# Leaving out some of GpSimd's clears between row gathers in a two-layer graph kernel

## The chip, the cores and the metric

The kernel runs on one core of one Trainium2 chip. The metric is the device time of one execution in microseconds. The core's engines run side by side, each through its own queue in order: TensorE (PE; its weight loads are shown as PEld), VectorE (DVE), ScalarE (ACT), GpSimd (POOL) and SyncE (SP). They wait for each other through semaphores. Time before: 2917.17 us, the median of 14 runs (2896.22 to 2936.71).

## The reference

16 graphs of 1024 nodes with 64 features each. Layer 0 adds a small network over `adj @ x` and normalizes. Layer 1 thins each node's neighbours and takes, feature by feature, a weighted sum of three quantiles over the neighbours that stay; then comes a network of two matrices and a normalization.

```python
# layer 0
messages = einsum('bij,bjh->bih', adjacency, h)
dh = tanh(concat([h, messages]) @ W1 + b1) @ W2 + b2
x = layernorm(x + dh)
# layer 1: which neighbours stay
nb = (adj > 0) & ~eye;  m = nb.sum(-1);  rank = cumsum(nb) - 1
skip = where(m > 10, (m + 1) // 2, 1)
removed = nb & (skip > 1) & mask & ((rank + 1) % skip == 0)
valid = adj_with_self_loops & ~(removed | removed.T)
# layer 1: quantiles of each feature over the valid neighbours
sv = sort(where(valid, x[neighbour], big))
agg = sum(w * interpolated(sv, tau) for tau, w in ((.25, .25), (.5, .5), (.75, .25)))
y = relu((x + agg) @ W1 + b1) @ W2 + b2
x = layernorm(x + y * mask)
```

## The kernel before, in words

The function `sparse` does all the work for inputs within its limits. (`general` is a slower form that runs only if a flag says that the input is outside; it did not run here.)

The graphs are taken in six sets: one, one, two, four, four and four graphs (sets 0 to 5). The nodes of a set are put in order of their number of neighbours, most first, and cut into tiles of 128 nodes, one node to a partition. The front does this for one graph after another: VectorE scores the adjacency tiles (`score`), ScalarE counts, TensorE transposes tiles and forms the messages, layer 0 follows (its rows go to tables in DRAM), and `places` finds each node's place in the order (`perm`). Then the heads of a set, its nodes with most neighbours, are fetched (`permuted`), their lists of neighbours made on VectorE, the removed neighbours picked, and the removals scattered by GpSimd into the tables (`table<-removes`).

After that the kernel goes through units, 47 in all. A unit is a tile, or up to four, with the same room for neighbours; `index4_8` in what follows is the unit of set 4 that begins with tile 8. For each unit:

- `fetches` calls `fetch_rows` (line 1124): for each neighbour place GpSimd issues one indirect DMA, a gather, that brings for each of 128 nodes the row (66 floats) of one neighbour into the tile `X`. After every third gather GpSimd clears a scratch tile of 128x384 bytes, `pause`, that nobody reads.
- `prepare`: VectorE and ScalarE put large values in empty places and find the quantile's weights.
- `sort`: VectorE runs a sorting network over the neighbour places, `tensor_tensor` with min or max between `X` and a second tile `Y`, so both inputs are in SBUF.
- `sum_up` and `finish`: ScalarE weights the sorted places, TensorE adds them up and applies the network, VectorE normalizes, and GpSimd scatters the result (`out_dram<-y`) with an indirect DMA.

There are four `X` tiles, so GpSimd may be up to four units ahead. Lists for later tiles of a set are made while units run; their `permuted` fetches are on GpSimd's queue too, two buffers at a time. The nodes with most neighbours of all (hubs) have units of their own. The two greatest classes, with 50 and 156 gathers (tiles `pair` and `X0`, here the great hubs), are fetched by `great_fetches` and sorted by `great_units`. They use memory that the front frees, and their lists (`hub_list`, `hub_sc`, then `hub_ix`) are made on VectorE once the heads of all sets are done.

The order of instructions on each engine is fixed when the program is built. The work is written as 19 jobs, generators that yield between steps (`run_jobs`). A planner, `Board`, keeps for each engine the modelled time at which it is free, and for each tile when it is written and read. Every call of an instruction goes through the class `Engine`, which adds a modelled cost: 1600 ns for an indirect DMA on GpSimd, 1.2 ns a byte for a clear (461 ns), and for VectorE 145 ns and a cycle an element. At each step the job that can start first by this model, with a bias for each job, goes on. So a changed cost or a left-out instruction on one engine can change the order on every engine. All calls pass through one helper, so nearly every instruction has the same line in the profile (316); it is told apart by its tiles.

Of the kernel before, what the change touches and what calls it, by code (L numbers as in the profile page):

```python
# [228 lines left out]
class Board:  # L229


    def __init__(self):
        self.free = dict.fromkeys("VATGS", 0.0)
        self.written, self.read = {}, {}
        self.mark = 0.0
        self.moved = 0.0
        self.table = None


class Engine:  # L240
# [34 lines left out]
    def __getattr__(self, name):  # L275
        op, board, key = getattr(self.engine, name), self.board, self.key

        def timed(*args, **kw):
            out = kw.get("out", args[0] if args else None)
            rest = list(args[1:] if "out" not in kw else args) + list(kw.values())  # L280
            func = next((a for a in rest if isinstance(a, type(AF.Tanh))), None)
            ins = [a for a in rest if isinstance(a, bass.AP) and a is not out]
            outs = [out] + [a for k, a in kw.items() if k == "accum_out" and a is not None]
            for k in ("in_offset", "out_offset"):
                if kw.get(k) is not None:
                    ins.append(kw[k].ap)
            start = board.free[key]
            for t in ins:
                if t.space != DRAM:
                    start = max(start, board.written.get(t.tensor.name, 0.0))  # L290
            for t in outs:
                if t.space != DRAM:
                    start = max(start, board.read.get(t.tensor.name, 0.0))
            cost = self.cost(name, out, ins, dict(kw, func=func))
            end = start + cost
            board.free[key] = end
            if key != "G" and "dma" in name:
                big = out if out.space != DRAM else ins[0]
                size = big.free_nbytes() * big.partition_size()
                board.moved = max(board.moved, start + LANDS) + size / 200  # L300
                end = board.moved + LANDS
                board.free[key] = start + cost
            elif key == "G" and "dma" in name:
                big = max([out] + ins, key=lambda t: 0 if t.space == DRAM else t.free_nbytes())
                size = big.free_nbytes() * big.partition_size()
                board.moved = max(board.moved, end) + size / 200
                end = board.moved + 2 * LANDS
            else:
                end += 100
            for t in ins:  # L310
                board.read[t.tensor.name] = max(board.read.get(t.tensor.name, 0.0), end)
            for t in outs:
                if t.space != DRAM:
                    board.written[t.tensor.name] = max(board.written.get(t.tensor.name, 0.0), end)
            board.mark = max(board.mark, end)
            return op(*args, **kw)  # L316

        return timed
# [47 lines left out]
def sparse(ctx, tc, x, adj, nodemask, w1a, b1a, w2a, b2a, w1b, b1b, w2b, b2b, consts, out,  # L366
# [5 lines left out]
    board = Board()  # L372
    V, A, T, GP, SY = (Engine(e, k, board) for e, k in zip(
        (nc.vector, nc.scalar, nc.tensor, nc.gpsimd, nc.sync), "VATGS"))
# [30 lines left out]
    pause = cp.tile([P, PAUSE], U8, name="s_pause")  # L405
# [718 lines left out]
    def fetch_rows(u, src):  # L1124

        X, n = u["X"], 0
        for k, cap in enumerate(u["caps"]):
            SY.dma_start(X[:, 0, k, :], u["own_rows"][k])
            for d in range(1, cap + 1):
                GP.indirect_dma_start(out=X[:, d, k, :], out_offset=None, in_=src,  # L1130
                                      in_offset=bass.IndirectOffsetOnAxis(
                                          ap=u["index"][k][:, d - 1:d], axis=0))
                n += 1
                if n % 3 == 0:
                    GP.memset(pause, 0.0)
                    yield "G", 0

    def check_limits(pool):
# [55 lines left out]
    def fetches(pool):  # L1194
        for i, (si, c, what) in enumerate(plan):
            yield "G", lambda i=i, si=si: i in units and done["heads"] > si
            if i >= XBUFS:
                yield "G", lambda i=i: done["free"] > i - XBUFS
            u = units[i]
            u["X"] = pool.tile([P, u["caps"][0] + 1, len(what), W], F32, tag="X", name="X",  # L1200
                               bufs=XBUFS)
            src = table
            if c is None:
                src = early[si] if si < len(early) else tables[SETS[si][0] // 4]
            elif c > 3:
                src = tables[0]
            yield from fetch_rows(u, src)
            done["fetch"] += 1
# [38 lines left out]
    def great_fetches():  # L1247


        yield "S", lambda: "pool" in late  # L1250
        pool = late["pool"]
        check_limits(pool)
        for c in (1, 0):
            late[c] = yield from hub_lists(pool, c, [0], "great_sc")
        for c in (1, 0):
            u = late[c]
            D = u["caps"][0] + 1
            yield "G", 0
            if c:
                pair = pool.tile([P, 2, D, 1, W], F32, tag="Y0", name="pair")  # L1260
                u["X"], u["Y"] = pair[:, 0], pair[:, 1]
            else:
                u["X"] = pool.tile([P, D, 1, W], F32, tag="X0", name="X")
            yield from fetch_rows(u, table)
            late["fetched"] = c
# [566 lines left out]
```

## Time and profile before

| what | value |
|---|---|
| median of 14 runs | 2917.17 us (2896.22 to 2936.71) |
| the profiled execution | 2935.83 us, span 2934.1 us |
| gathers into X and pair | 1238 |
| scatters and list fetches on GpSimd: out_dram, permuted | 122, 128 |
| clears (s_pause) | 402, mean 439 ns, 176.4 us in all |
| first `perm` to last | 74 to 1113 us |
| last head's removals scattered | 1307 us |
| great hubs: 50 gathers, then 156 | 1360 to 1428, 1429 to 1705 us |
| last gather ends | 2863 us |

The page is of one execution; its times are not the median's. A row of the page names engine, operation, output tile and inputs, then the count, the busy time, the mean of one, and the idle time of the engine before it with what ended it. "Issue" is a gap in which the engine waited for nothing that the profile shows. The indirect DMAs have rows on POOL for the time in which GpSimd prepares them; their landing is another matter.

The sort steps' own rows overlap a little, since VectorE starts one step before the one ahead has ended. A 128x256 step has a row of 0.42 us and follows the one before it by about 0.34.

### The profile page before, as it was taken

The page shows a single profiled execution, that of the slowest core. Times are in us where ns is not written, and L with a number is a line of the kernel's source. Part 1 is how long each engine was busy: PE and PEld are TensorE (multiplying, and loading weights), DVE is VectorE, ACT ScalarE, POOL GpSimd, SP SyncE. Part 2 cuts the span into 40 slices and gives each one's busy share as a digit, 9 for nine tenths or more (in the row PEclk, how much of TensorE's full clock was granted, in tenths as well). Part 3 has the DMA queues.
Part 4 walks back from the last instruction along what each step waited for, and adds up shares of the span by engine and source line. Part 5 has one row for each costly group of instructions (what it writes and reads, how often), then busy time and mean ns, then how long its engine had stood idle before and what let it go on. Part 6 is the DMA issues. An engine that isn't in the chain of part 4 may idle for free.

```text
span 2934.1 us, 23546 instructions
## 1 busy us (share of the span) xinstructions
PE 1260.9 (43%) x4992; PEld 790.3 (27%) x4992; DVE 1987.4 (68%) x5189; ACT 1248.0 (43%) x3739; POOL 1924.7 (66%) x1955
## 2 busy tenths in 40 slices
PE   6786757756686674210233002221124421103376
PEld 4453434434443332200123001121012221102155
DVE  3467877575678686769994005878889786688752
ACT  5685676554777554222222026222225322123364
POOL 1035835777524575767688883878888888888882
PEclk9897867856786776555555555555555555555555
DMA  7476545234445342311111111122111122121110
GB/s 242 150 211 168 154 128 151 56 85 113 126 140 163 94 122 52 64 29 35 20 22 22 25 26 44 38 46 51 23 23 24 26 51 43 28 58 27 24 25 8
DMA packets 158610, 215.63 MB, mean 73 GB/s; under 512 B 88524, under 2 KB 88716, under 8 KB 158460
## 3 DMA queue, kind: packets, MB, share of 16 engines
q0 software_dynamic: 56192, 87.29, 14.5%
q1 hardware_dynamic: 83836, 93.20, 11.2%
q10 hardware_dynamic: 18432, 33.56, 3.1%
q14 instruction: 108, 0.88, 0.1%
q8 instruction: 42, 0.69, 0.1%
HBM read 157.21 MB, written 56.70 MB: 73 GB/s over the span
## 4 chain that ended last, share of the span: by engine, by line
POOL 38%; PE 16%; DVE 16%; issue 15%; ACT 9%; DMA 3%; another core or an unknown queue 2%; SPq 0%; POOLq 0%; DVEq 0%; ACTq 0%
POOL X L316 30%; PE pn L316 6%; ACT junk L316 5%; POOL s_pause L316 4%; POOL out_dram L316 3%; PE pt L316 3%; DVE Y L316 3%; PE pa L316 3%; DVE X L316 2%; ACT X L316 2%; PE rows L316 2%; DVE hub_list L316 2%; DVE score L316 2%; DVE hub_sc L316 1%
## 5 line engine op out<-in xcount | busy, mean ns | idle before, releaser
L316 POOL DMA_INDIRECT X<-table,index x711 | 808.0, 1136 | 210.9 <-issue 188.8
L316 ACT ACTIVATE X<-X,fill 128x64 f32<-128x64 f32 x1188 | 304.9, 336 | 498.1 <-DVE fill L316 415.3
L316 PE MATMUL pa<-X,s_half_ident 128*128 128x64 f32 (+3 forms) x636 | 202.4, 467 | 561.3 <-ACT X L316 461.9
L316 POOL DMA_INDIRECT X<-table,hub_ix x262 | 317.5, 1212 | 69.7 <-issue 69.4
L316 POOL DMA_INDIRECT permuted<-score_rows,ids x128 | 143.7, 1122 | 325.1 <-DMA early<-s_rows 112.3
L316 PE MATMUL pa<-Y,s_half_ident 128*128 128x64 f32 (+2 forms) x522 | 174.1, 478 | 369.0 <-ACT Y L316 223.7
L316 PEld LDWEIGHTS pa<-X,s_half_ident 128*128 128x128 f32 x636 | 141.7, 298 | 623.1 <-ACT X L316 511.2
L316 POOL DMA_INDIRECT X<-early,index x215 | 224.9, 1046 | 93.3 <-issue 56.0
L316 PE MATMUL pn<-aT,x_sb 128*64 128x256 f32 x1024 | 279.8, 421 | 5.1 <-issue 4.8
L316 DVE TENSOR_TENSOR Y<-X 128x512 f32<-128x512 f32 (+11 forms) x414 | 248.2, 625 | 8.9 <-PE pt L316 6.4
L316 ACT ACTIVATE X<-X,wt 128x64 f32<-128x64 f32 x614 | 162.9, 336 | 195.7 <-DVE X L316 195.3
L316 POOL DMA_INDIRECT out_dram<-y,out_ids x122 | 142.4, 1167 | 145.5 <-DVE y L316 80.3
L316 PEld LDWEIGHTS pa<-Y,s_half_ident 128*128 128x128 f32 x522 | 118.6, 302 | 418.2 <-ACT Y L316 250.9
L316 PE MATMUL pt<-s_ident,a_sb 128*128 128x128 f32 x1024 | 166.5, 309 | 135.4 <-ACT aT L316 82.4
L316 DVE SCALAR_TENSOR_TENSOR score<-a_sb,s_desc 128x1024 f16<-128x1024 f32 x128 | 155.0, 1222 | 94.5 <-DMA score_rows<-score 47.2
L316 DVE TENSOR_TENSOR X<-Y 128x256 f32<-128x256 f32 (+10 forms) x377 | 212.4, 582 | 2.5
L316 ACT ACTIVATE Y<-Y,wt 128x64 f32<-128x64 f32 x530 | 141.9, 336 | 146.0 <-DVE Y L316 125.1
L316 ACT COPY aT<-pt 128x512 f32<-128x512 f32 x256 | 138.7, 583 | 142.0 <-PE pt L316 65.4
L316 PEld LDWEIGHTS pt<-s_ident,a_sb 128*128 128x128 f32 x1024 | 136.4, 197 | 180.0 <-ACT aT L316 97.0
L316 POOL MEMSET s_pause<- 128x384 uint8 x402 | 176.4, 439 | 3.0 <-remote 2.8
L316 PEld LDWEIGHTS pn<-aT,x_sb 128*64 128x64 f32 x1024 | 143.0, 150 | 107.3 <-issue 49.7
L316 ACT ACTIVATE junk<-keys,nkey 128x1024 bf16<-128x1024 f32 x128 | 142.5, 1113 | 26.6 <-DVE nkey L316 6.5
(181 smaller groups left out, 2904.5 us busy)
## 6 DMA issues: line engine op xcount, KB each, us to landing
a_sb<-in_adj_dram SPq DMA_DIRECT2D x128, 512.0 KB
score_rows<-score ACTq DMA_DIRECT2D x128, 256.0 KB
X<-table,index POOLq DMA_INDIRECT x711
score_rows<-s_rows SPq DMA_DIRECT2D x16, 264.0 KB
table<-s_rows SPq DMA_DIRECT2D x16, 264.0 KB
X<-table,hub_ix POOLq DMA_INDIRECT x262
x_sb<-in_x_dram SPq DMA_DIRECT2D x16, 256.0 KB
own_rows<-permuted SPq DMA_DIRECT2D x122, 33.0 KB
```

The lines of the kernel that those rows point to most:

```text
L316: return op(*args, **kw)
```

## The change

The planner keeps a list of the modelled start and end of every `tensor_tensor` on VectorE. Where a clear would be issued it looks at the 6000 ns that end at VectorE's modelled time. If `tensor_tensor` fills more than half of them, and GpSimd's modelled time is less than 6000 ns ahead of VectorE's, the clear is left out. Otherwise it is issued as before. The job still yields after every third gather.

```diff
@@ class Board
         self.table = None
+        self.pairs = []
+
+    def paired(self, span=6000):
+        now, total = self.free["V"], 0.0
+        for start, end in reversed(self.pairs):
+            if end <= now - span:
+                break
+            total += end - max(start, now - span)
+        return self.free["G"] - now < span and total > 0.5 * span
@@ class Engine, timed
             board.free[key] = end
+            if key == "V" and name == "tensor_tensor":
+                board.pairs.append((start, end))
@@ fetch_rows
                 n += 1
                 if n % 3 == 0:
-                    GP.memset(pause, 0.0)
+                    if not board.paired():
+                        GP.memset(pause, 0.0)
                     yield "G", 0
```

## The prediction

> **What bounds the kernel now.** I read the page's engine rows and slices first, then windows over the stages, then single instructions. The profiled execution took 2935.83 us (span 2934.1). It lies near the top of the 14 runs, 0.64% above their median of 2917.17, so I work out a difference against it and put that difference on the median.
>
> ```profile
> span 2934.1 us, 23546 instructions
> PE 1260.9 (43%) x4992; PEld 790.3 (27%) x4992; DVE 1987.4 (68%) x5189; ACT 1248.0 (43%) x3739; POOL 1924.7 (66%) x1955
> ...
> DVE  3467877575678686769994005878889786688752
> ...
> POOL 1035835777524575767688883878888888888882
> ...
> POOL 38%; PE 16%; DVE 16%; issue 15%; ACT 9%; DMA 3%; another core or an unknown queue 2%; SPq 0%; POOLq 0%; DVEq 0%; ACTq 0%
> ```
>
> Over the whole span no engine is full, but from slice 24 on GpSimd (POOL) stands at 8 in every slice but the last, and it leads the chain that ended last. The stages (columns: PE, PEld, DVE, ACT, POOL busy, with instruction counts):
>
> ```profile
> 0.00:1080.00 1080.00, 743.59 (x3277) 442.87 (x3277) 715.19 (x2019) 669.57 (x1545) 525.20 (x564) 0.77 0.50 141
> 1080.00:1360.00 280.00, 79.81 (x373) 56.44 (x372) 205.19 (x681) 87.33 (x278) 187.13 (x202) 0.58 0.25 50
> ...
> 1429.00:1565.00 136.00, 54.46 (x143) 32.77 (x144) 130.99 (x279) 48.86 (x190) 104.53 (x85) 0.53 0.10 19
> 1565.00:1707.00 142.00, 18.10 (x76) 14.44 (x74) 7.14 (x27) 12.50 (x48) 114.80 (x140) 0.52 0.12 25
> ...
> 1830.00:2863.00 1033.00, 302.87 (x906) 198.96 (x906) 806.77 (x1905) 325.54 (x1281) 857.09 (x809) 0.52 0.18 35
> ```
>
> Two facts follow. Before 1080 us GpSimd waits a lot; afterwards it hardly does. In 1830 to 2863 it is busy 857 of 1033 us, and nearly all the rest is a gap of 0.30 us ahead of each gather, which is issue and not a wait. Counting only gaps above that 0.30 us, it is idle for 431 us before 1080, 50 in 1080 to 1360, 14 in 1429 to 1565, 39 in 1707 to 1830 and 6 until 2863. So from 1080 on the end moves with the sum of GpSimd's work, until about 71 us of sums and output remain after the last gather (2863). VectorE (DVE) follows: it is at 78% in the last long stage and idle in 1565 to 1707.
>
> **What a clear costs.** In a stretch without sorting:
>
> ```profile
> 1642.10 0.94 POOL L316 DMA_INDIRECT X<-table,hub_ix  x1 [0.30 <-issue]
> 1643.35 0.95 POOL L316 DMA_INDIRECT X<-table,hub_ix  x1 [0.30 <-issue]
> 1644.30 0.43 POOL L316 MEMSET s_pause<- 128x384 uint8 x1
> 1644.89 0.95 POOL L316 DMA_INDIRECT X<-table,hub_ix  x1 [0.16 <-issue]
> ```
>
> From 1642.10 to 1643.35 is one gather to the next, 1.25 us. With a clear between, 1643.35 to 1644.89, it is 1.54 us. So a clear costs 0.29 us and not the 0.44 us of its row: its own time takes the place of one 0.30 gap, and the gap after it is 0.16.
>
> **Part 1, clears removed.** In the two programs' GpSimd orders there are 402 clears before and 172 after, 230 fewer. By stage of the new order: 25 fewer ahead of the great hubs' gathers (units up to index3_5), 34 of 68 fewer among the great hubs' 206 gathers, 12 fewer in index3_8, 3_12 and 3_16, and 159 of 188 fewer from index3_20 to the end. The first 25 lie mostly before 1080 where 431 us of waits cover them: nothing, and a gain of 7 us if that cover were gone. The other 205 x 0.29 = **-60 us**.
>
> **Part 2, what VectorE does to gathers.**
>
> ```profile
> L316 POOL DMA_INDIRECT X<-table,hub_ix x56 | 83.7, 1494 | 14.9 <-issue 14.9
> L316 POOL MEMSET s_pause<- 128x384 uint8 x18 | 7.9, 438 | 0.0
> ```
> ```profile
> L316 POOL DMA_INDIRECT X<-table,hub_ix x100 | 95.1, 951 | 25.9 <-issue 25.9
> L316 POOL MEMSET s_pause<- 128x384 uint8 x34 | 14.8, 436 | 0.0
> ```
> ```profile
> 1527.83 19.34 DVE L316 TENSOR_TENSOR pair<-pair 128x256 f32<-128x256 f32 x63
> 1527.93 0.44 POOL L316 MEMSET s_pause<- 128x384 uint8 x1
> 1528.53 17.67 POOL L316 DMA_INDIRECT X<-table,hub_ix  x1 [0.16 <-issue]
> ```
>
> The first pair is 1429 to 1565 with VectorE sorting, the second 1565 to 1707 with it idle, the third one gather held for 17.67 us by 63 sort steps. Gathers are stretched (1494 against 951 ns); clears are not (438 against 436). Sort steps are not slowed by gathers: a 128x256 step takes 421 ns with a gather beside it throughout (231 of them) and 421 with GpSimd idle (27). So VectorE neither gains nor loses here. Does a clear spare the next gather some of the stretch? Over all unit gathers with sorting beside at least 90% of their time, the first after a clear takes 1543 ns (115 of them), the second 1389 (125), the third 1308 (123). It does not, so I count the 0.29 in full; the bound on the other side is that half of it comes back as longer gathers (+30).
>
> The Trainium skill (SBUF — State Buffer, section Who interferes with whom) says that a VectorE instruction with two SBUF inputs locks out a GpSimd instruction that reads SBUF, but not one that only writes. That fits these rows and speaks against the change: the clear is the one thing in this queue that a sort cannot delay, so its time might only become waiting for the port. By that rule alone, with all 205 given back, the sum below would be +30 and 2947 us; by the row it is -30.
>
> **Part 3, the planner moves work.** Removing clears changes the planner's GpSimd time and so every engine's order. The largest move: the great hubs' gathers (50 and 156 rows) now stand ahead of index3_8, 3_12 and 3_16 (90 gathers). They need VectorE's lists of the great hubs, behind the last heads of set 5. Before, GpSimd had those 90 gathers to do meanwhile (58+54+37 us of fetch spans in 1191 to 1360). Now it has little, and in its queue everything stands behind the great gathers: the 90 rows that VectorE sorts next, list fetches, and scatters of results.
>
> When are the lists ready? I add each VectorE instruction at its mean duration along both orders. From the last placement tile (1113 us) to the 50 rows' index (1350) VectorE had 178 us of work in 237 us, 75% busy. In the new order it is 129 us, as the sorts of index3_1 to 3_5 are put after it, and the placement comes some 13 us sooner. At 75%: 1100 + 172 = 1272. Bounds: 1229 with VectorE always busy, 1350 if nothing comes sooner. GpSimd has 95 us of work for 1080 to 1272 (280 less 50 idle less some 135 for the 90 gathers, their clears, stretch and scatters), so it idles 97 instead of 50: **+47 us**, between +4 and +125. The second index comes 47 us of VectorE work later, 63 at 75%, as long as the 50 gathers take (50 x 1.25 + 14 x 0.29 = 67): no second wait.
>
> Coming back: the 39 us idle in 1707 to 1830 is mainly one wait, for list buffers while VectorE was held at the great hubs' first step:
>
> ```profile
> POOL permuted L316 <- DVE lists L316: 37.5, 3, 30.3
> ```
>
> With 90 more gathers (113 us) ahead of that point VectorE can catch up: **-30 us**, between 0 and -39. The 14 us wait for a scatter stays.
>
> The 90 gathers change company: their stretch was 9 us in 1170 to 1360; beside the great hubs' sort I take the late stage's rate (151 us of stretch over 587 gathers from 1707 on, 0.26 each): 23 us, so **+14 us**, between 0 and +41 (the 0.56 of 1429 to 1565).
>
> SyncE's issues for each unit's own rows go with the units and the list transfers change place alike; SyncE is no share of the chain (SPq 0%). ScalarE has four table loads fewer and TensorE the same instructions; both are at 43% or below: nothing. VectorE has the same instructions. If its cover went, that is if VectorE were late for gathered units, the late stage has 1033 - 807 = 226 us of room, against 46 us (159 x 0.29) by which that stage shrinks.
>
> **Sum.** -60 + 47 - 30 + 14 = -29 us: 2936 becomes 2907, and 2917 becomes **2888** (0.990).
>
> **The rivals.**
> A, the sum: about 2888, its own range 2862 to 2910. Chance 0.50.
> B, the great hubs' gathers take the place of the clears as the wait. GpSimd stands at the first of the 50 gathers until VectorE has the lists; each us later than 1272 is one us at the end. From 1301 on nothing is gained, from 1316 on the kernel is slower by over 0.5%. At 1335, with VectorE's waits unshortened: -29 + 63 = +34, 2951 us. For it: VectorE's waits in 1080 to 1360 are partly for other engines. Against: GpSimd fetches the heads sooner with nothing between. 0.22.
> C, half of the clears' time comes back as stretched gathers: -29 + 30, 2918 us. For it the 17.67 us row, against it the places after a clear. 0.15.
> D, the planner's new order suits: lists at 1229, the list wait gone, no added stretch: -60 + 4 - 39 + 0 - 7 = -102; I put it at 2830. 0.13.
> That the change does nothing is excluded by the count of clears; 42% stay.
>
> **How the numbers follow.** About 0.5% (15 us) is what a measurement can tell from no change. Faster: 0.42 of A, all of D, 0.03 of C = 0.58. Same: 0.08 of A, 0.09 of C, 0.03 of B = 0.20. Slower: 0.19 of B, 0.03 of C = 0.22. Range: 2838 to 2955, from just short of D's 2830 to just past B's 2951, some 0.10 left out on either side.
>
> **What would show it.** Clears 172; gather to gather 1.25 us still; the 50-row gathers starting near 1272 with GpSimd idle before them, the 156-row ones ending near 1595 (1705 before); index3_20 starting near 1744 (1707 + 47 + 14 - 46 x 0.29, less 11 for 8 scatters that move behind it); no list wait of 30 us behind it; the last gather some 30 us sooner. I am wrong if the 50 rows start after 1301 (step 3), if the gathers' mean in the late stage rises above 1.3 us from 1.23 (step 2), or if VectorE gets over 90% busy there.

## The result, and the profile after

The changed kernel takes 3049.3 us (median of 10 runs, 3028.82 to 3071.45) where the kernel before takes 2920.2 us beside it: a ratio of 1.0466 [1.0435, 1.0497]. It is slower by 4.7%, and the time lies above the range that was given. Measured again beside the kernel before (e20 below), it came to 1.0421 [1.0341, 1.0500].

The page of the changed kernel, the same rows as were shown of before:

```profile
span 3055.3 us, 23339 instructions
PE 1270.5 (42%) x4992; PEld 792.3 (26%) x4992; DVE 1982.6 (65%) x5189; ACT 1247.8 (41%) x3735; POOL 1775.0 (58%) x1725
...
DVE  3467777556748467699900096768886686578732
...
POOL 1037635752337573456868737676778576866751
...
POOL 20%; DVE 15%; issue 10%; another core or an unknown queue 4%; PE 4%; ACT 3%; DMA 2%; DVEq 0%; POOLq 0%; ACTq 0%
```

The clears are gone (230 instructions and 150 us of GpSimd's busy time), the other engines have the same work but for four table loads of ScalarE, and the span is 121 us longer. GpSimd (POOL) no longer stands at 8 through the last third, and VectorE (DVE) did not take its place: both wait. Now the stages, by the new order's own boundaries (columns: PE, PEld, DVE, ACT, POOL busy, with counts): up to the great hubs' 50 gathers, those, the 156, the 90 gathers of index3_8 to 3_16, and from index3_20 to the last gather. The line of before that answers to the last one stands behind it.

```profile
1080.00:1324.00 244.00, 82.43 (x368) 50.99 (x368) 177.44 (x618) 72.54 (x186) 107.32 (x113) 0.61 0.27 63
1324.00:1391.00 67.00, 2.81 (x13) 2.81 (x14) 64.95 (x97) 3.21 (x14) 54.06 (x64) 0.50 0.16 30
1391.00:1650.00 259.00, 55.01 (x227) 46.41 (x226) 139.44 (x357) 47.07 (x190) 190.29 (x185) 0.53 0.12 24
1650.00:1819.00 169.00, 19.43 (x38) 8.76 (x38) 70.09 (x105) 71.32 (x271) 101.36 (x112) 0.50 0.12 20
1819.00:2973.00 1154.00, 336.73 (x920) 205.69 (x920) 833.18 (x2041) 369.73 (x1422) 832.43 (x736) 0.51 0.18 35
```
```profile
1707.00:2863.00 1156.00, 318.62 (x938) 206.20 (x938) 843.76 (x2017) 391.48 (x1528) 923.97 (x887) 0.52 0.18 35
```

Two things are to be seen. The last stage, with 159 clears fewer and 92 us less of GpSimd's work, takes 1154 us against 1156: nothing was gained. And it begins at 1819 and not at 1707, so the loss of 112 us is made before it. Behind it, sums and output take 82 us instead of 71.

What GpSimd waits for from 1800 to 2980 (total, times, longest):

```profile
POOL out_dram L327 <- DVE y L327: 152.9, 9, 41.4
```

Before, the long wait here was the one for lists (37.5 us), and waits for results in 1707 to 2865 were these:

```profile
POOL out_dram L316 <- DVE y L316: 6.7, 2, 4.8
```

The list wait is gone as forecast, and a larger one stands in its place: a scatter at the head of GpSimd's queue waits for a result that VectorE has not finished, and all gathers behind it wait too. In the front (200 to 1324) GpSimd also waits more; the first two lines are of after, the third is the second's counterpart of before (200 to 1360):

```profile
POOL X L327 <- PE pa L327: 79.7, 5, 34.6
POOL permuted L327 <- DVE pairs L327: 50.3, 5, 21.1
```
```profile
POOL permuted L316 <- DVE pairs L316: 15.7, 4, 4.3
```

The gathers did not become longer. Their groups in after (busy us, mean ns of one, then idle time before them):

```profile
L327 POOL DMA_INDIRECT X<-table,index x711 | 787.7, 1108 | 214.5 <-issue 204.6
L327 POOL DMA_INDIRECT X<-table,hub_ix x262 | 301.7, 1152 | 82.4 <-issue 74.9
```

And in before:

```profile
L316 POOL DMA_INDIRECT X<-table,index x711 | 808.0, 1136 | 210.9 <-issue 188.8
L316 POOL DMA_INDIRECT X<-table,hub_ix x262 | 317.5, 1212 | 69.7 <-issue 69.4
```

So neither the clears' time nor a longer gather holds the answer.

### The profile page after: what moved, and what is told of

Same layout as the page of the kernel before. It is cut to its first block, busy times and chain, and to the rows that moved or that the text cites. A ratio compares the mean times of both kernels' runs of the same rounds, so it can differ in the third digit from the quotient of the medians.

```text
span 3055.3 us, 23339 instructions
## 1 busy us (share of the span) xinstructions
PE 1270.5 (42%) x4992; PEld 792.3 (26%) x4992; DVE 1982.6 (65%) x5189; ACT 1247.8 (41%) x3735; POOL 1775.0 (58%) x1725
## 4 chain that ended last, share of the span: by engine, by line
POOL 20%; DVE 15%; issue 10%; another core or an unknown queue 4%; PE 4%; ACT 3%; DMA 2%; DVEq 0%; POOLq 0%; ACTq 0%
POOL X L327 16%; DVE Y L327 3%; DVE X L327 3%; DVE pair L327 2%; PE pa L327 2%; POOL out_dram L327 2%; ACT X L327 2%; DVE hub_list L327 2%; DMA X<-table,index 1%; DVE hub_sc L327 1%; POOL permuted L327 1%; PE py L327 1%; ACT Y L327 1%; DVE pre L327 1%
## 5 line engine op out<-in xcount | busy, mean ns | idle before, releaser
L327 POOL DMA_INDIRECT X<-table,index x711 | 787.7, 1108 | 214.5 <-issue 204.6
L327 PE MATMUL pa<-X,s_half_ident 128*128 128x64 f32 (+3 forms) x636 | 211.9, 474 | 670.0 <-ACT X L327 421.4
L327 POOL DMA_INDIRECT X<-table,hub_ix x262 | 301.7, 1152 | 82.4 <-issue 74.9
L327 DVE TENSOR_TENSOR X<-Y 128x256 f32<-128x256 f32 (+9 forms) x377 | 213.2, 582 | 8.9 <-issue 2.5
L327 ACT ACTIVATE junk<-score 128x1024 bf16<-128x1024 f16 x128 | 135.0, 1055 | 39.0 <-DVE score L327 38.5
```

## The experiments

There were 18 runs in five groups; the kernels of a group ran on one chip beside the kernel before, whose medians there were 2904.93, 2781.99, 2932.36, 2916.09 and 2941.21 us. All ratios are to before of the same group; a profile is one execution of a kernel and can lie off its median (before's 18 us above, e2's 25 us below). "Order" is the order of instructions on each engine. Each text that stands as a quotation is what was expected of a run before it was made; T1 to T9 in them are names of theories.

### Order against clears

The kernel after differs from before in two things at once: clears are missing, and the order is another. Four kernels take these apart.

e1_old_order: the planner is charged for each clear that is left out, so the order of before stays on all engines, and 221 clears are not issued.

```
 if board.paired(): planned_clear()      # adds PAUSE * 1.2 to free["G"]
 else: GP.memset(pause, 0.0)
```


> The instructions of every engine stand in the order of the kernel before; only 221 of the 402 clears are not issued (the planner still charges them). Theory T1, the order is what costs and a clear in itself costs 0.29 us on a busy GpSimd: some 200 clears after 1080 us at 0.29 give -58 us at most, and some of it goes into new waits for results that come no sooner: 0.975 to 0.995 of before. Rival T2, the clears themselves help (gathers without clears hinder the other engines, or come back as stretch): 1.03 to 1.05, like the changed kernel. Rival T3, GpSimd's time in the late stage is made up by waits whatever is removed: 0.995 to 1.005.

e2_new_order_all_clears: the order of after, with every left-out clear issued past the planner.

```
-if not board.paired(): GP.memset(pause, 0.0)
+if board.paired(): nc.gpsimd.memset(pause, 0.0)
+else: GP.memset(pause, 0.0)
```


> The order of the changed kernel on every engine, with all 402 clears issued (230 of them unknown to the planner). T1: as slow as the changed kernel or slower, 1.045 to 1.065 of before. T2 (the clears themselves help): back near before, 0.99 to 1.01. T3: the same as the changed kernel, 1.04 to 1.05, since the new waits shrink by what the clears take.

e3_late_only and e4_early_only: clears are left out only from index3_20 on (158 fewer), or only ahead of it (71 fewer).

```
e3: if not (u.get("late") and board.paired()): GP.memset(pause, 0.0)
e4: if u.get("late") or not board.paired():    GP.memset(pause, 0.0)
```


> Clears are left out, and the planner told so, only from unit index3_20 on; up to there every order is that of before. In the changed kernel the stretch from index3_20's first gather to the last gather took 1154 us against 1156 before although 159 clears fewer were issued, so T1 expects 0.995 to 1.01 of before, with new waits of GpSimd for scatters of results of 80 us or more. If the late stage of the changed kernel lost only by what it inherited from the stages before it, this gives the expected gain of 46 us: 0.98 to 0.99.

> Clears are left out, and the planner told so, only up to index3_20 (the great hubs' gathers among them); every clear from there on is issued and planned. T1: the 112 us that the changed kernel was behind at index3_20 stay, 1.03 to 1.05 of before. If that loss is made up later by a planner that has clears to give, 1.00 to 1.02.

| kernel | clears | order | ratio |
|---|---|---|---|
| e1 | 181 | before | 1.0032 [0.9986, 1.0079] |
| e2 | 402 | after | 1.0531 [1.0463, 1.0599] |
| e3 | 244 | before up to index3_20 | 1.0083 [1.0046, 1.0119] |
| e4 | 331 | after up to index3_20 | 1.0386 [1.0334, 1.0438] |

The loss needs no missing clear: e2 issues all 402 and is as slow as after. It lies in the order, and most of it in the order up to index3_20: e4 is 1.039, e3 only 1.008 (their product is 1.047, the result, though their late orders are not that of after). In e2's profile index3_20 starts at 1821 us, as in after (1819) and not as in before (1707). Its last stage then takes 1126 us, with some 16 us of waits of GpSimd above its 0.30 us gaps; in after, with 159 clears fewer there, it takes 1154 (1135 in e20, the same kernel) with 110. But the second finding is as important. With the order held fixed, 221 clears less bring nothing (e1), where the prediction's 0.29 us each would make 64 us or 2%. What was freed is waiting again: in the stage from index3_20 to the last gather GpSimd's waits above its 0.30 us gaps are 85 us in e1 and 46 in before, and beside the great hubs 44 and 14.

### How little it takes to change the order

e8_front_only leaves out 25 clears, all in units up to index3_5. e9_one_clear leaves out one single clear, in index1_2, and tells the planner. e16_another_single_clear leaves out another single one, in index2_2.

```
e8:  if not (u.get("front") and board.paired()): GP.memset(pause, 0.0)
e9:  if left_out or not board.paired(): GP.memset(pause, 0.0)
     else: left_out.append(1)
e16: as e9, in the unit of set 2 that begins with tile 2
```


> Clears are left out, and the planner told so, only in units up to index3_5: 25 clears, together worth 7 us. The order of every engine is that of the changed kernel until the great hubs' gathers, which stand ahead of index3_8. If the loss is the planner's new order of the front: 1.025 to 1.045, nearly all of e4's 1.039. If the clears that are missing among the great hubs' gathers and after make the loss: 0.995 to 1.01.

> One clear is left out, in unit index1_2, worth 0.29 us, and the planner told so; every order changes behind it. If the planner's order is a matter of chance once its times move, the result may lie anywhere within some per cent of before, 0.98 to 1.04, and not at 1.00. If only the leaving out of many clears moves units against each other, 0.997 to 1.003.

> One clear is left out, in unit index2_2 some 200 us later than in e9, and the planner told so. With e9 at 1.021: if a single clear shuffles the planner's order with an outcome of chance, anything in 0.98 to 1.04, other than e9's; if leaving out a clear always leads to the same worse order, 1.015 to 1.025; if only e9's place was bad, 0.997 to 1.003.

Measured: e8 1.0321 [1.0242, 1.0401], e9 1.0206 [1.0121, 1.0291], e16 0.9892 [0.9844, 0.9939]. One clear of 0.44 us in the front moves the end by +61 us, another by -26 us. This is no effect of a clear: the planner is greedy, each of its choices depends on modelled times, and a shift of 461 modelled ns sends it down another path. The order that it then finds is close to a draw, and the change drew a bad one.

What is bad in it can be read in part. In each of the four new orders that cost 2% or more (after with e2, e14 and e11, whose other engines keep its order, and e4, e8 and e9) the 206 gathers of the great hubs stand ahead of the 90 of index3_8 to 3_16; in those of e3 (1.008) and e16 (0.989) they stand behind them, as in before. In e9 they start at 1180 us, 87 us sooner than in e6 of the same group (1267; order of before, later scatters), and yet index3_20 starts 51 us later (1656 against 1605), since the 90 gathers now come behind. GpSimd's waits up to that point, counted above the 0.30 us gap, are 445 us in e9 and 384 in e6. So in the order of before the 90 gathers seem to fill time in which GpSimd has nothing else, and behind the great hubs they are work of their own; no run moved the 90 alone. For the profiles of after and before the same count gives 658 and 495 us.

e14_new_order_lists_first tried one suspect in the front: in after, list fetches stand behind gathers that wait for a free `X`. It is after with the 15 gathers of index2_12 issued behind the next four list fetches.

```
+if (si, c, what[0]) == (2, None, 12): kept["after"] = 4   # its gathers go out after four permuted()
```


> The changed kernel, except that the 15 gathers of unit index2_12, which in its trace wait 28 us for a free X tile with four list fetches behind them, are issued after those list fetches; other engines' order is unchanged. Theory T6: the front is late because list fetches stand behind gathers that wait for an X tile, and VectorE waits for the lists (21.6 us at 873 to 894): 1.025 to 1.04 of before against 1.047. Rival: the front is late for reasons spread over many places, 1.042 to 1.05.

Measured 1.0493 [1.0431, 1.0555], no better than after. That theory fell; which of the front's waits begins the delay stays open.

### Why missing clears bring nothing: scatters first

The waits of 152.9 us for `y` suggested a cheap cure: issue the scatters of a result up to 12 gathers later on GpSimd, so that nothing stands behind them (three `y` buffers; the other engines' order unchanged).

```
+if board.hold is not None and key == "G":
+    board.hold.append((op, args, kw)); return None
...
+scatters.append((gathered["n"] + AFTER, calls))    # AFTER = 12
```

e5 is e1 with it, e6 before with it (all 402 clears), e11 after with it, and e12 e5 with no clear at all.

> As e1 (the order of before, 221 clears not issued), but each unit's scatters of its result are issued up to 12 gathers (some 15 us) later on GpSimd than planned, and three y buffers instead of one; the order on the other four engines is unchanged. Theory T4: in e1 GpSimd, quicker than planned, comes to a scatter before VectorE has the result and holds the gathers behind it (its waits for y rose from 99 to 149 us), which takes what the clears gave. Then this gives the gain back: 0.975 to 0.99. Rival T5: GpSimd and VectorE wait for each other in turn through the units' data and a later scatter only moves the wait to another instruction: 0.995 to 1.01, as e1.

> The control for e5: the order of before, all 402 clears issued, the scatters up to 12 gathers later. Before has few waits for y between 1080 us and the last gather (33 us), so T4 expects 0.985 to 1.0, and e5 below it by some 1 to 2%. T5: 0.995 to 1.005, and e5 the same.

> The changed kernel with its order and its 172 clears, and each unit's scatters up to 12 gathers later (three y buffers), as in e5. In the changed kernel GpSimd waits 153 us for y between index3_20's start and the last gather. T4 expects most of that back: 1.005 to 1.025 of before, and no gain for what the front lost. T5: 1.04 to 1.05.

> The order of before, none of the 402 clears issued (the planner charges them all), scatters up to 12 gathers later. Beside e5 (0.977) it leaves out 181 clears more, of which 94 lie before index3_16's end where GpSimd mostly waits, 31 in the stretch of the great hubs' gathers with VectorE idle: T4 expects 0.96 to 0.975. If the remaining clears help somebody, 0.977 or more.

| kernel | clears | group | ratio |
|---|---|---|---|
| e5 | 181 | 2 | 0.9770 [0.9712, 0.9829] |
| e6 | 402 | 2 | 0.9976 [0.9948, 1.0005] |
| e11 | 172, order of after | 3 | 1.0570 [1.0523, 1.0617] |
| e12 | 0 | 3 | 1.0374 [1.0326, 1.0422] |

e5 looked like a version that beats both kernels, and in that group the left-out clears paid (e5 against e6: 53 us for 221 clears, 0.24 us each, near the prediction's 0.29). Then e11 and e12 came out 3 and 6% above what was expected. In e12 more of the same clears are left out in the same order than in e5, and it was slower, not faster (but in another group). The traces show something that goes with it: VectorE stands still where its data is there. I counted its gaps over 0.6 us from 1750 to 2900 us that the trace puts down to no known releaser, without the first instruction of a unit, which waits for a gather to land (one profile of each kernel):

```
full clears nearly all issued late:  e2 5, e16 10, before 13, e4 19 us
left out late:                       e1 28, e3 49, after 67, e11 89, e14 137 us
no clear at all:                     e12 179 us
second group (e5, e6, e8, e9):       0 us
```

This count leans on what the trace records, and most traces lack a part of the semaphore updates (last section). A count that doesn't: gaps over 0.6 us between two sort steps that follow each other on VectorE, in the same stretch. It gives 0 us for before, e4, e16 and all four of the second group, 1 for e2, 17 for e1, 30 for after, 34 for e3, 56 for e14, 68 for e12 and 76 for e11. So the gaps are there, whatever the trace lacks.

### The breaks themselves

So there were three suspects: the missing breaks between gathers, the later scatters, and the chip of the group. e19 is e12 again, e18 is e5 again, e20 is after again, and e17 has all 402 clears, each of 16 bytes a partition in place of 384, and later scatters.

```
-GP.memset(pause, 0.0)
+GP.memset(pause[:, :16], 0.0)
```


> The kernel of e12 again (order of before on all engines, no clear at all, scatters of results later), now on one chip with 181 clears (e18), with 402 short ones (e17) and with the changed kernel (e20). Theory T7 (gathers without a break hold up the other engines: in runs of gathers with no clear between them, finished instructions release their followers late, and VectorE stands still with its data ready; such gaps of VectorE over 0.6 us came to 13 us in 1750 to 2900 of before, 67 of after, 179 of e12): on a chip that shows such gaps in the front 1.03 to 1.045, with 120 to 220 us of gaps; on a chip that shows none (as in e5 and e6) 0.95 to 0.97. Rival T8 (the later scatters are at fault where e12 ran): this run and e18 are slower than before alike, within 1%.

> The kernel of e5 again (order of before, 181 clears, scatters later). T7 on a chip with such gaps: between e17 and e19, 0.99 to 1.01, VectorE's gaps 30 to 90 us; on a chip without: 0.97 to 0.985. T8: 1.02 to 1.04 on a chip with gaps.

> Order of before, all 402 clears, each of 16 bytes a partition in place of 384, scatters later. T7a (a break is enough, however short): VectorE's gaps in 1750 to 2900 at most 25 us on any chip, and 402 clears that are shorter by some 0.3 us of their 0.44: 0.965 to 0.985. T7b (the length of the pause counts): gaps of 50 us or more and 1.00 to 1.03 on a chip that shows them in the front. T8: like e18 and e19.

> The changed kernel itself, on the chip of e17 to e19. Order and missing clears together: 1.04 to 1.055 on a chip with gaps; on a chip without, only the order costs and the missing clears pay: 1.00 to 1.025 (T7). T8: 1.04 to 1.055 on any chip.

Then the two edits each by itself: e21 is before with short clears and nothing else, e22 is e6 again.

> The kernel before with one edit: each of its 402 clears writes 16 bytes a partition in place of 384, so it takes some 0.13 us in place of 0.44. Order of every engine unchanged, scatters where they were. T7b (the pause itself is what lets the other engines' releases through, its length counts): front later by 20 to 60 us, VectorE's gaps of 1750 to 2900 at 60 us or more, 1.01 to 1.04. Rival T9 (a clear is only GpSimd's time, as the prediction priced it; the later scatters made e17 and e19 slow): 0.97 to 0.995.

> The kernel of e6 again: order of before, all 402 clears in full, scatters later. T7b: within 1% of before, 0.99 to 1.01, VectorE's gaps of 1750 to 2900 at most 25 us. T9: slower than before like e18 or more, 1.015 to 1.04.

| kernel | clears | scatters | group | ratio | VectorE's gaps, us (between sort steps alone) |
|---|---|---|---|---|---|
| e18 | 181 | later | 4 | 1.0190 [1.0115, 1.0264] | 76 (44) |
| e19 | 0 | later | 4 | 1.0315 [1.0206, 1.0425] | 61 (56) |
| e17 | 402 short | later | 4 | 1.0438 [1.0363, 1.0513] | 161 (57) |
| e20 | 172, order of after | as before | 4 | 1.0421 [1.0341, 1.0500] | 54 (30) |
| e21 | 402 short | as before | 5 | 1.0288 [1.0252, 1.0324] | 53 (53) |
| e22 | 402 | later | 5 | 1.0205 [1.0161, 1.0250] | 6 (7) |

e18 and e19 alone left it open: e18 was slower than T7 had it, e19 only 1.2% above e18, and its gaps (61 us) half of the smallest expected.

e21 decides. It is the plainest run of all. Every engine has the order of before and the same number of instructions; the clears take 134 ns instead of 439, which is 123 us less on the engine that was said to bound the kernel; and the kernel is 87 us slower. The full clear is worth more than it costs. That refutes the prediction's price.

What the short clear takes away can be read from its rows. In e21 two unhindered gathers with a clear between them start 1.25 us apart (median of 200), and two without start 1.25 apart (509); in before it is 1.54 (213) and 1.25 (503). A clear of 0.13 us only fills the gap that is there anyway. So in the spacing of its gathers e21 is a kernel without clears, and what it lacks is 0.29 us behind each third gather (e17 and e19, one with short clears and the other with none, are 1.044 and 1.032, and their intervals meet). A break that is longer than none and shorter than 0.29 us was not tried, so T7a (a break is enough, however short) stays open. T7b's sign and time came out (1.029 in its 1.01 to 1.04); its gaps, 53 us, fell short of its 60. The later scatters are a second, separate loss of 2% (e22, where T7b had expected none and T9 a loss like this), which was not there in e6 of the second group; T8 alone cannot be, since e21 has no later scatters. e17 has both and stands near their product (1.050).

The late stage of e21, to be held against the line 1707 to 2863 of before above:

```profile
1741.00:2946.00 1205.00, 314.21 (x929) 203.54 (x930) 843.74 (x2017) 395.34 (x1528) 849.67 (x888) 0.52 0.18 34
```

VectorE's 2017 instructions are busy for 843.74 us against 843.76, the same work. GpSimd has 74 us less to do. The stage takes 49 us more. The time is between VectorE's instructions. Here is a stretch of e21 in which VectorE sorts one unit beside the gathers of the next (start us, duration us, engine; idle time before it in brackets):

```profile
2554.04 0.94 POOL L316 DMA_INDIRECT X<-table,hub_ix  x1 [0.30 <-issue]
2554.44 0.43 DVE L316 TENSOR_TENSOR Y<-Y,X 128x256 f32<-128x256 f32 x1 [1.18 <-DVE X L316]
...
2555.29 1.10 POOL L316 DMA_INDIRECT X<-table,hub_ix  x1 [0.18 <-issue]
2555.86 0.29 DVE L316 TENSOR_TENSOR Y<-Y 128x128 f32<-128x128 f32 x1 [0.28 <-DVE Y L316]
2556.70 0.94 POOL L316 DMA_INDIRECT X<-table,hub_ix  x1 [0.30 <-issue]
2557.24 0.23 DVE L316 TENSOR_TENSOR Y<-Y 128x64 f32<-128x64 f32 x1 [1.09 <-DVE Y L316]
2557.95 0.94 POOL L316 DMA_INDIRECT X<-table,hub_ix  x1 [0.30 <-issue]
2558.67 0.56 DVE L316 TENSOR_TENSOR X<-Y 128x384 f32<-128x384 f32 x1 [1.20 <-DVE Y L316]
2558.88 0.14 POOL L316 MEMSET s_pause<- 128x16 uint8 x1
2559.19 0.95 POOL L316 DMA_INDIRECT X<-table,hub_ix  x1 [0.18 <-issue]
```

and one of before, with the same unit being sorted and the same hub unit gathered:

```profile
2506.05 1.43 POOL L316 DMA_INDIRECT X<-table,hub_ix  x1 [0.30 <-issue]
2506.55 0.48 DVE L316 TENSOR_TENSOR Y<-Y 128x320 f32<-128x320 f32 x1
2507.07 1.29 DVE L316 TENSOR_TENSOR X<-Y 128x512 f32<-128x512 f32 x2
2507.78 1.42 POOL L316 DMA_INDIRECT X<-table,hub_ix  x1 [0.30 <-issue]
2508.39 1.09 DVE L316 TENSOR_TENSOR Y<-X 128x768 f32<-128x768 f32 x2
```

In before VectorE's steps follow each other without a gap and the gathers give way (1.42 us). In e21 it is the other way round: the gathers keep their 0.94, and VectorE, which waits for nothing but its own last step, gets in one step or a few and stands still again. From 2550 to 2586 us it has 17 gaps over 0.6 us, 23 us in all, beside 24 DMAs of GpSimd of which 22 took less than 1 us. The 111 sort steps in a row from 2534.73 on are the same instructions as the 111 from 2502.82 on in before; they take 71 us from first to last, against 41.

The trace tells which part is late: not VectorE but the word that its last step is done. The step at 2554.44 waits for a semaphore that VectorE's own instructions raise. The step ahead of it is over at 2553.26, the semaphore's update is recorded at 2554.42, and VectorE goes on 0.02 us later. In e21 the trace has such an update for 27 of the 39 gaps between sort steps, a median of 1.08 us after the end of the step; in e5, whose trace lacks almost none, an update follows the end of its instruction by 0.01 us, 0.61 at the longest. Nor do the late updates keep the beat of the gathers, 1.25 us: the steps behind a wait start at 2554.44, 2555.86, 2557.24 and 2558.67, about 1.40 us apart, and in the whole trace of e21, as in those of after, e11, e12 and e17, the starts behind gaps between sort steps lie close to multiples of 0.70 us apart (1.40, 2.10, 2.80). What keeps this beat no run tells.

Then results come late and scatters wait for them:

```profile
POOL out_dram L316 <- DVE y L316: 117.5, 7, 33.1
```

That late releases are the way from the short clear to the longer stage is read from two traces of different groups, in which the unexplained gaps grew by 40 us and those between sort steps by 53, where the stage grew by 49. That the shorter clears cost the time is shown by e21 itself. Why releases come late beside gathers that follow each other without the 0.29 us is open; a longer pause than that of before was not tried, nor was the order of before with its scatters in place and no clear at all.

No version came out that beats both kernels on every chip. e16 beat before by 1.1% in its group by luck of the order; e5 won 2.3% in one group and lost 1.9% in another.

## Why the prediction was wrong, point by point

1. "From 1080 on the end moves with the sum of GpSimd's work." This is the step that failed first. It holds for the trace of before in the main (where the prediction read 8 throughout, from slice 24 on, the row of slices has a 3 and a 7; the slice of the 3 holds the list wait), but it says only who was busy, not who would wait once the work shrinks. In after GpSimd's waits above its 0.30 us gaps come to 110 us in the last stage, 46 before.

2. "So a clear costs 0.29 us", 205 of them 60 us. As GpSimd's time this was right, and in one group e5 against e6 gave 0.24 each. As the kernel's time it was wrong: 221 clears less at a fixed order gave 1.0032, and 123 us less of clears (e21) cost 87 us. Nor is a clear's worth one figure, since the 221 of e1 cost nothing. The last stage should have taken 1090 us by the prediction's own steps; it took 1154.

3. "VectorE neither gains nor loses here." The reading that went wrong was of rows: a sort step takes 421 ns with a gather beside it and without, and that is still so. The price is not in a step's duration but in the gap ahead of it, which a mean over rows doesn't show. With clears every three gathers the gap is hardly there in before, so its trace couldn't show what their absence does. The bound that was set (+30 us, "half of it comes back as longer gathers") looked on the wrong engine: gathers became shorter (1108 against 1136 ns). The same goes for the rule drawn on there, the Trainium skill's SBUF — State Buffer, section Who interferes with whom, that a sort locks out a gather. The section also says that issue order decides which of the two engines blocks. The stretch of before, with its gathers of 1.42 us, fits a lock; in e21's VectorE is not locked out but starts 0.02 us after a release that comes late. Its sentence that TensorE and ScalarE wait on no one does not cover e12's rows (below), where a release comes late too.

4. The planner's move: +47 us, with the great hubs' start at 1272 and bounds from +4 to +125. The sign, the place and the mechanism (GpSimd stands at the first of the 50 gathers) were right, the size was not: they started at 1324. The term that failed is "the placement comes some 13 us sooner": the last placement tile came at 1164 instead of 1100, the time from there to the start (160 against 172) was about right. That is 52 us. The same order with all clears (e2) has it at 1158, so it is the order's doing. The term rested on adding up VectorE's durations along the new order at the old order's 75%, and so on nothing in the front being late for another reason. From there to index3_20 it took 495 us instead of 472, another 23, with one scatter wait of 41 us at 1812 in it.

5. "-30 us" for the list wait: gone as forecast, but waits for results stand in its place (152.9 us), which the prediction had left at one wait of 14 us.

6. Sum of the misses: 52 + 23 + 64 (1154 - 1090) + 11 (tail) = 150 us on top of 2907, which makes 3057, the profiled execution's time. So by stages half of the error lies before index3_20 and half behind it. By causes the order weighs more: e2, with every clear in place, costs 5.3%, some 155 us, where the prediction's terms for the order add up to +31 (47 - 30 + 14). Leaving out 230 clears in that order then gave back 0.6% or nothing (1.0466 against 1.0531, from different groups, whose intervals meet), where -60 us, 2%, had been counted.

Of the rivals, B named the first part with its place and its threshold (slower from a start at 1316). At 1324 it gives +23 us, and no rival had the rest; C let half of the clears' time come back, but as longer gathers, which did not occur. Of the prediction's three signs of being wrong the first came, a start after 1301. The gathers' mean did not rise, and VectorE stayed at 72% (833 of 1154) in the last stage, so that neither of the other two alarms went off. An alarm for VectorE idle with its data ready was missing.

The range failed for a reason that can be stated: it treated the new order as the old one plus a few moves. e9 and e16 show that one clear alone swings the time from -1.1 to +2.1% through the order. Any change of a modelled cost in this kernel draws a new schedule, and that spread belongs into the range.

## What to carry to other kernels

An instruction that computes nothing can still do work: before a pause on one engine is priced at its own duration, shorten it at a fixed order and look at the gaps of its neighbours, not at their durations. Where a greedy planner sets the order, separate what an edit does from what its schedule does (charge the planner for what is left out), and count the schedule as a draw with its own spread. A gain measured once is to be repeated at another time and on another chip before it is believed.

## What the runs showed of the hardware that was not expected

Gathers by GpSimd and sort steps by VectorE side by side have two outcomes: either VectorE runs through and a gather is held (17.67 us in the prediction's row), or gathers run at 0.94 us and VectorE stands still between steps, since the update of its own semaphore comes late, in e21's gaps 1.08 us after the step's end at the median. Full clears of 0.44 us after each third gather kept VectorE's unexplained gaps of the late stage at 5 to 19 us in five profiles (before, e2, e4, e16, e22); with those clears left out or short they came to 28 to 179 us in eleven, though not in step with the number left out (e18 76, e19 61).

In such stretches other engines are let go late too. In e12, TensorE's last matmul into `pa` is over at 1971.5, and ScalarE, which waits for it, goes on at 1989.97; GpSimd issued indirect DMAs 1.25 us apart up to 1984.9. TensorE ran nothing between 1971.5 and 1990.24, but the updates of its semaphore come at 1972.18, 1983.38 and 1988.97, then seven of them, some 0.04 us apart, from 1989.70 to 1989.95; ScalarE starts 0.02 us behind the last. So the updates had piled up and came in one go 5 us after GpSimd had stopped issuing. The lines of TensorE and of ScalarE in 1969 to 1992:

```profile
1970.81 0.69 PE L332 MATMUL pa<-Y,s_half_ident 128*128 128x64 f32 x2 [0.71 <-remote]
1990.24 0.42 PE L332 MATMUL pu<-s_ident,agg 128*64 128x128 f32 x1 [18.74 <-ACT agg L332]
```
```profile
1989.97 0.21 ACT L332 COPY agg<-pa 128x64 f32<-128x64 f32 x1 [27.97 <-remote]
```

The second group was different for all its kernels, and why stays open. The kernel before took 2781.99 us there, 4 to 5% less than in the other four groups; its four kernels have no unexplained gap of VectorE from 1750 to 2900; and of VectorE's 4040 semaphore updates in e5 the trace records 4038, against 3040 in e22 of the last group. What holds the releases up elsewhere did not act there, and there missing clears paid. A chip with the same number as in the second group showed the gaps in the fourth, so it isn't settled that the chip is what differs. Every profile with gaps lacks a fifth or more of these updates, but before, e2, e4, e16 and e22, which have hardly any, lack as much; no run tells whether the recording of the trace has a part in the delays.
